# Two empty items between the first one-hots and the first tile of each compaction in a two-layer graph kernel

## The chip, the cores and the metric

The kernel runs on one core of a Trainium2 chip. Its time is the device time of one execution in microseconds (us), and the profile used here is one execution recorded by the hardware profiler. Engines are named as in the profile: PE is the matrix engine (PEld its weight loads), DVE the vector engine, ACT the scalar engine, POOL the general engine (GpSimd), SP the engine that issues most DMAs. A line number such as L612 is a line of the kernel before the change.

## The reference, cut to what matters

Two layers work on x (3327 nodes, 128 features) and a sparse weighted adjacency matrix of 3327 x 3327. The first layer multiplies by the normalised matrix and its transpose and normalises each row. The second is attention with an adjacency bias, and takes nearly all of the time:

```python
q = (x @ Wq.T).reshape(d, n, h)          # d = 128 heads, n = 3327, h = 8
k = (x @ Wk.T).reshape(d, n, h)
v = (x @ Wv.T).reshape(d, n, h)
a = jnp.einsum('dnh,dmh->dnm', q, k) * scale
a = a + spatial_encoding + edge_encoding  # both are adj
a = jax.nn.softmax(a, axis=2)
out = jnp.einsum('dnm,dmh->dnh', a, v)
out = out.reshape(n, h * d) @ Wo.T
x = layernorm(x + out)
```

So there are 128 independent heads, each with a 3327 x 3327 score matrix of inner length 8, an exponential of every score, and a product with 8 values and a row of ones.

## The kernel before, in words

**The main loop.** The heads go in 32 groups of four (g = 0 to 31). For each group the loop at L1396 takes 7 blocks of up to 512 queries and, in each, 26 tiles of 128 keys. The unit of the loop is a *half*: PE makes the scores of two heads for one tile and one block (L1416, tile `e_ps`), ACT takes their exponentials (L1436, tile `es`; L1438 for the last block, where one exponential takes all four heads), and PE multiplies the exponentials of the tile before by the values (L1364, tile `o`). A group has 6 x 52 + 26 = 338 halves, the whole loop 10,816. Every half has one exponential, so the loop runs at best at the pace of ACT.

**What runs beside it.** The maximum of each score row, needed ahead of the exponentials, is not computed from all 3327 keys. The keys of largest norm are picked (a top 1024 and a further 1024) and packed densely; PE multiplies queries by the packed keys and DVE takes maxima. This work of the group ahead is cut into *items*, a stream written by `stream_of` (L929). An item is one of:

- "maxima": two matmuls (L1034) and two DVE maxima over 512 columns (L1043);
- "queries": rebuilds a few query rows for the second 1024 keys (L1018, L1027);
- "hots" and "fill", the *compaction* of the packed keys for the next group, written by `fills` (L766). A "hots" item makes four one-hot tiles with DVE (L612, bf16, 128 x 336). A "fill" item multiplies a tile of keys by four one-hots on PE (8 matmuls, L621), and then makes the four one-hots of the tile after the next on DVE. So two sets of one-hots always lie ahead. A compaction has two "hots" items and 30 "fill" items, the first 15 for the first 512 packed keys, the other 15 for the second 512. There are 30 compactions, one for each of groups 2 to 31, each running while the group before is in the main loop;
- None: an empty item, which takes its place in the stream and emits nothing. Before the change these stand only where the stream has to wait, most of them beside group 30, which has no compaction.

**Pacing.** `next_item` (L1335) takes one item of the stream. Before each half the loop compares the number of items taken with `due(halves)` (L1390), a straight line through the points in `wanted` (L1385), whose slope comes from the number of items of a group. When an item is due (`busy`, L1426), the half carries it, its PE work between the scores and the exponential. When it is not, the half instead lets the small generators in `running` take a step (`turn`, L974), and may let the slow background work take a step (`next(beside)`, L1458; `next(choosing)`, L1456). After the first groups a busy half lets none of these step. So the number of items, empty ones included, decides how many steps the background work gets.

**The background work.** `choosing` selects the keys of largest norm for later groups (beside groups 1 to 6). `beside` runs `neighbours` (L1064) and then `closing` (L1203). `neighbours` treats the exact scores along the edges, node tile by node tile (26 tiles): it gathers rows with indirect DMAs (L1084), takes inner products on DVE (L1094, L1098), then exponentials on ACT, and then on POOL, for each of up to 16 neighbours, a product of gathered values with a share (L1152 for the first neighbour, L1155 for the others) and a sum (L1156). I call such a product with its sum a *value product*. `closing` finishes one tile of 128 output rows at a time (26 tiles): it loads the sums, scales them (L1254 to L1285), transposes them (L1293), multiplies by Wo (L1307) and normalises. What is left of `beside` when the main loop ends runs after it (L1465), with nothing else to do.

POOL's other large job is in `fix` (L809): eight masked products over queries for each pair of heads (L848, then sums L853 to L858).

**Order.** The order of instructions on PE, ACT, DVE, POOL and SP is exactly the order in which this Python code emits them (L1333). Each engine runs its own list in order and waits only for data and buffers, so POOL can be ahead of the loop or behind it. Steps of `beside` cost credits in units of a half (`spend`, `earn`), with which the code keeps DVE and POOL from falling far behind.

Of the kernel before, what the change touches and what calls it, by code (L numbers as in the profile page):

```python
# [52 lines left out]
TCUTS = TOP // NB  # L53
# [10 lines left out]
POOL_BEHIND = 4.0  # L64
DEEPEST = 12.0
READY = 500
MARGIN = 60


def window(t):  # L70
    return EXPECTED * t // NT - BEFORE
# [7 lines left out]
def gnn_layers(ctx: ExitStack, tc: tile.TileContext, x, adj, adjt, w_in, w_out, wq, wk, wv, wo, out):  # L79
# [89 lines left out]
    with ExitStack() as c0:  # L169
# [435 lines left out]
        def tiles_of_fill(u):  # L605
            return [t for t in range(NT) if window(t) < (u + 1) * NB and window(t) + REACH > u * NB]
# [27 lines left out]
        def spread(g, packed):  # L634
            pairs = coming["s", g] = []
            for j in range(GH):
                x, y = j // 2, j % 2
                for slot, parts in KROWS:
                    r = 64 * (1 - y) + H * slot
                    pairs.append((k_kept[g % 2][r : r + H * parts, x, :], packed[32 * j : 32 * j + H * parts, :]))  # L640
# [103 lines left out]
    with c_att as c1:  # L744
# [21 lines left out]
        def fills(g, at, parts):  # L766
            packed = side.tile([P, KEPT], BF16, name="packed")
            state = {}
            order_of = [(u, t) for u in range(TCUTS) for t in tiles_of_fill(u)]
            yield "hots", g, at, order_of[0][1], state  # L770
            yield "hots", g, at, order_of[1][1], state
            for (u, t), after in zip(order_of, [*order_of[2:], None, None]):
                tiles = tiles_of_fill(u)
                yield "fill", g, at, parts, packed, u, t, after, t == tiles[0], t == tiles[-1], state
            spread(g, packed)
# [153 lines left out]
        def stream_of():  # L929
# [13 lines left out]
            parts = split_keys(side, coming_keys[1])  # L943
            maxima_of(2, 1)
            yield from fills(2, coming_keys[0], parts)
            yield from of_rest(1, 0)
            yield from of_rest(1, 1)
            yield from of_top(2, 0)
            for g in range(2, NG):
                if g + 1 < NG:  # L950
                    coming_keys = load_choice(side, g + 1)
                    maxima_of(g + 1, 0)
                yield from of_top(g, 1)
                if g + 1 < NG:
                    maxima_of(g + 1, 1)
                    parts = split_keys(side, coming_keys[1])
                    yield from fills(g + 1, coming_keys[0], parts)
                else:
                    for _ in range(30):
                        yield None  # L960
                yield from of_rest(g, 0)
                if g + 1 < NG:
                    yield from of_top(g + 1, 0)
                else:
                    for _ in range(40):
                        yield None
                yield from of_rest(g, 1)
# [365 lines left out]
        with tc.manual_schedule(engines={ENG.PE, ENG.Activation, ENG.DVE, ENG.Pool, ENG.SP}):  # L1333
# [47 lines left out]
            total = halves = 0  # L1381
            steps = NT * (2 * len(BLOCKS) - 1)
            top, rest = NT * TCUTS, 2 + ROOM * (KCUTS - TCUTS)
            fill = 2 + sum(len(tiles_of_fill(u)) for u in range(TCUTS))
            wanted = [(0, taken), (2 * steps - MARGIN, taken + 4 * top + 4 * rest + 2 * fill + top)]  # L1385
            for g in range(3, NG):
                wanted.append((steps * g - MARGIN, wanted[-1][1] + 2 * (top + rest) + fill))
            wanted.append((steps * NG - MARGIN, wanted[-1][1] + 40))

# [6 lines left out]
            for g in range(NG):  # L1396
                for b, (n0, w) in enumerate(BLOCKS):
# [9 lines left out]
                    for t in range(NT):  # L1407
                        pt = P if t < NT - 1 else P - (NP - N)
                        e = [None] * GH
                        for x0 in range(0, 2, per):  # L1410
# [41 lines left out]
                            if not busy and t and credit["dve"] > 0:  # L1452
                                if halves >= READY and len(chosen_all) < len(LATE):
                                    if "fill" not in held:
# [250 lines left out]
```

## Time and profile before

| what | value |
|---|---|
| median of 3 runs (12162.31 to 12165.54) | 12163.84 us |
| the profiled execution, own time | 12176.24 us |
| its span in the profile | 12174.6 us |
| first and last start of an exponential (L1436, L1438) | 1226.0 us, 12096.4 us |
| end of the main loop's exponentials | 12097.6 us |
| median distance between starts of exponentials | 0.92 us |
| sum of what these distances have over 0.92 us | 920 us |
| ACT es, L1436, x9984 | 9476.1 us busy |
| DVE one-hots, L612, x3840 | 1302.7 us busy, 406 ns mean |

The profiled execution is 12.4 us (0.1%) longer than the median. The distances are those between the starts of successive exponentials in the trace: 10,816 of them, in the order in which the kernel emits them, so each can be put to its half, group and item. In a group without special trouble (groups 7 and 8) they sum to 14.9 us over 338 x 0.92 us.

### The profile page before, as it was taken

The numbers are of one execution on the slowest core, as the hardware profiler recorded it, in microseconds if no ns is written. First come the engines' busy times: TensorE is split into PE (matmuls) and PEld (weight loads), VectorE is DVE, ScalarE is ACT, GpSimd is POOL, SyncE is SP. The second block draws the span as 40 slices with busy tenths as digits, with TensorE's granted clock in tenths as the row PEclk, the third lists the DMA queues.
The fourth block names the chain that finished last, engine by engine and source line by source line (L and its number), as shares of the span: only waits on it lengthen the run. The fifth ranks groups of instructions, "written<-read, shape, count | busy, mean of one in ns | idle before, by whom it ended". The sixth has DMA issues, their size and how long they took to land.

```text
span 12174.6 us, 238129 instructions
## 1 busy us (share of the span) xinstructions
PE 11268.4 (93%) x90213; PEld 2996.4 (25%) x90246; DVE 9384.3 (77%) x18234; ACT 10771.0 (88%) x11299; POOL 3377.5 (28%) x4098
## 2 busy tenths in 40 slices
PE   6647999999999999999999999999999999999997
PEld 3321222222222222222222222222222222222222
DVE  9678787878787788788888887887888778777533
ACT  6431899999999999999999999999999999999996
POOL 0221111111111124444433334334343434211100
PEclk8765999999999999999999999999999999999998
DMA  6562444344441123222222222322222222233112
GB/s 231 159 161 67 40 42 41 37 37 38 39 38 23 19 58 76 61 56 61 61 65 64 64 52 64 72 56 70 60 55 61 62 65 65 62 86 65 35 47 57
DMA packets 2237807, 783.23 MB, mean 64 GB/s; under 512 B 1854432, under 2 KB 2128355, under 8 KB 2229989
## 3 DMA queue, kind: packets, MB, share of 16 engines
q1 hardware_dynamic: 2154085, 436.67, 23.2%
q0 software_dynamic: 78816, 286.92, 7.4%
q10 hardware_dynamic: 3744, 44.29, 1.0%
q8 instruction: 712, 11.67, 0.4%
q14 instruction: 450, 3.69, 0.1%
HBM read 595.42 MB, written 187.86 MB: 64 GB/s over the span
## 4 chain that ended last, share of the span: by engine, by line
ACT 36%; PE 35%; DVE 13%; issue 13%; DMA 1%; SPq 1%; POOL 0%; ACTq 0%; DVEq 0%; POOLq 0%
ACT es L1436 34%; PE o L1364 17%; PE e_ps L1416 11%; DVE mx_top L1043 4%; PE m L1034 3%; DVE mx_rest L1043 1%; DVE hot L612 1%; DVE top_at L256 1%; ACT es L1438 1%; DVE top_w L255 1%; PE acc L246 1%; PE pr L693 1%; PE m L1307 1%; DVE o_sb L1373 1%; PE m L1189 0%
## 5 line engine op out<-in xcount | busy, mean ns | idle before, releaser
L1436 ACT ACTIVATE es<-e_ps 128x1024 f32<-128x1024 f32 (+1 forms) x9984 | 9476.1, 1023 | 729.4 <-PE e_ps L1416 446.7
L1364 PE MATMUL o<-es,v 128*9 128x512 f32 x46592 | 5766.4, 567 | 32.7 <-DVE o_sb L1373 32.2
L1043 DVE TENSOR_REDUCE mx_top<-m 128x1 f32<-128x512 f32 x6656 | 4255.7, 685 | 1200.6 <-PE m L1034 1178.9
L1416 PE MATMUL e_ps<-q_e,k_st 50*128 50x512 bf16 (+1 forms) x23296 | 4271.8, 371 | 227.3 <-ACT es L1436 77.2
L1416 PEld LDWEIGHTS <-k_st 50*128 50x128 bf16 (+1 forms) x23296 | 1408.3, 95 | 6261.3 <-issue 5780.4
L1043 DVE TENSOR_REDUCE mx_rest<-m 128x1 f32<-128x512 f32 x2048 | 1309.6, 684 | 356.3 <-PE m L1034 352.6
L1034 PE MATMUL m<-k_kept,q_m 48*128 48x512 bf16 x6656 | 1434.0, 386 | 110.4 <-DVE mx_top L1043 62.0
L612 DVE TENSOR_SCALAR hot<-hot_no,at 128x336 bf16<-128x336 bf16 x3840 | 1302.7, 406 | 221.6 <-PE m L621 205.5
L848 POOL TENSOR_TENSOR slot_each<-hits,whole_q 128x832 f32<-128x832 f32 x256 | 425.6, 1663 | 2893.1 <-DVE hits L833 2878.0
L1364 PEld LDWEIGHTS o<-es,v 128*9 128x9 f32 x46592 | 696.3, 88 | 1563.8 <-issue 1447.1
L1438 ACT ACTIVATE es<-e_ps 128x1020 f32<-128x1020 f32 x832 | 810.5, 1024 | 78.2 <-PE e_ps L1416 60.9
L1034 PEld LDWEIGHTS <-q_m 48*128 48x128 bf16 x6656 | 509.0, 144 | 159.0 <-issue 152.7
L1084 POOL DMA_INDIRECT near_rows<-kn_d,near x211 | 201.4, 954 | 1069.6 <-DVE prod L1094 1004.8
L1034 PE MATMUL m<-k_kept,slot_rows_q 48*128 48x512 bf16 x2048 | 443.1, 385 | 34.5 <-DVE mx_rest L1043 27.6
L802 POOL TENSOR_TENSOR slot_each<-whole_q 128x416 f32<-128x416 f32 x64 | 57.4, 897 | 1429.3 <-DMA whole_q<-qf_d 1378.2
L1156 POOL TENSOR_TENSOR acc<-acc,prod 128x1024 f32<-128x1024 f32 x185 | 430.3, 2326 | 14.5
L246 PE MATMUL acc<-a_t,x 128*128 128x512 f32 (+1 forms) x728 | 311.5, 585 | 63.0 <-DMA a_t<-in_adj_dram 43.0
L1155 POOL TENSOR_TENSOR prod<-near_rows,s 128x1024 f32<-128x1024 f32 x185 | 365.9, 1978 | 2.4
L621 PE MATMUL m<-hot,parts 128*24 128x168 bf16 (+9 forms) x7200 | 289.8, 230 | 40.5 <-DVE hot L612 40.2
L1084 POOL DMA_INDIRECT near_rows<-vn_d,near x211 | 206.9, 980 | 345.6 <-DVE prod L1094 295.6
L1094 DVE TENSOR_TENSOR prod<-qn,near_rows 128x512 f32<-128x512 f32 x422 | 296.2, 702 | 0.0
L853 POOL TENSOR_TENSOR slot_each<-slot_each 128x416 f32<-128x416 f32 x256 | 288.1, 1125 | 20.1
(308 smaller groups left out, 5914.5 us busy)
## 6 DMA issues: line engine op xcount, KB each, us to landing
q_m<-q_d SPq DMA_DIRECT2D x768, 52.0 KB
q_e<-q_d SPq DMA_DIRECT2D x2304, 16.0 KB
a_t<-in_adj_dram ACTq DMA_DIRECT2D x13, 1663.5 KB
a_t<-in_adj_dram SPq DMA_DIRECT2D x13, 1663.5 KB
a_t<-in_adjt_dram SPq DMA_DIRECT2D x13, 1663.5 KB
a_t<-in_adjt_dram ACTq DMA_DIRECT2D x13, 1663.5 KB
q_d<-parts SPq DMA_DIRECT2D x13, 1536.0 KB
k_d<-parts SPq DMA_DIRECT2D x13, 1536.0 KB
```

The source lines that it names most:

```text
L246: nc.tensor.matmul(acc[:, b, :w], x0[:, t, :], a_t[:, n0 : n0 + w], start=t == 0, stop=t == NT - 1)
L612: nc.vector.tensor_scalar(hot, hot_no, at[:, t, j : j + 1], None, op0=ALU.is_equal)
L848: nc.gpsimd.tensor_mul(each, hits[y][:, i : i + 4, :, None].to_broadcast(shape), whole_q[:, y, None].to_broadcast(shape),)
L1034: nc.tensor.matmul(banks[y], of[rows[y], tile_of], kept[rows[y], x, c * NB : (c + 1) * NB], start=True, stop=True,)
L1043: nc.vector.tensor_reduce(mx[:, i, y, c - c0 : c - c0 + 1], banks[y], axis=AX.X, op=ALU.max)
L1084: nc.gpsimd.indirect_dma_start(rows.rearrange("p d h -> p (d h)"), None, table, bass.IndirectOffsetOnAxis(ap=rows_at, axis=0))
L1155: nc.gpsimd.tensor_mul(prod, vg, share)
L1156: nc.gpsimd.tensor_add(acc[:, :, :H], acc[:, :, :H], prod)
L1364: nc.tensor.matmul(o[32 * j : 32 * j + VW, :w], v4[:pt, j, t, :], e[j][:pt], start=t == 0, stop=t == NT - 1,)
L1416: nc.tensor.matmul(bank[:pt, y, x * NB // per : x * NB // per + w], k[r, x0 + x, t * P : t * P + pt], q[r, x0 + x, :w], start=True, stop=True,
L1436: nc.scalar.activation(es[:pt, :, :w], bank[:pt, :, :w], AF.Exp, scale=2.0)
L1438: nc.scalar.activation(es[:pt].rearrange(shape, x=per)[:, :, :, :w], bank[:pt].rearrange(shape, x=per)[:, :, :, :w], AF.Exp, scale=2.0,)
```

## The change

Between the two "hots" items and the first "fill" item of each compaction, two empty items are put into the stream. The count `fill`, from which the due times are worked out, grows from 32 to 34, so that the line `wanted` allows for them. The instructions of the program are the same in number on every engine; their order among each other changes.

```diff
+CATCH_UP = 2
...
         yield "hots", g, at, order_of[0][1], state
         yield "hots", g, at, order_of[1][1], state
+        for _ in range(CATCH_UP):
+            yield None
         for (u, t), after in zip(order_of, [*order_of[2:], None, None]):
...
-            fill = 2 + sum(len(tiles_of_fill(u)) for u in range(TCUTS))
+            fill = 2 + CATCH_UP + sum(len(tiles_of_fill(u)) for u in range(TCUTS))
             wanted = [(0, taken), (2 * steps - MARGIN, taken + 4 * top + 4 * rest + 2 * fill + top)]
             for g in range(3, NG):
                 wanted.append((steps * g - MARGIN, wanted[-1][1] + 2 * (top + rest) + fill))
```

## The prediction, made before the result was known

> **What bounds the kernel now.** I read the page first, then the engine table in windows, then the trace exponential by exponential. The page:
>
> ```profile
> span 12174.6 us, 238129 instructions
> PE 11268.4 (93%) x90213; PEld 2996.4 (25%) x90246; DVE 9384.3 (77%) x18234; ACT 10771.0 (88%) x11299; POOL 3377.5 (28%) x4098
> L1436 ACT ACTIVATE es<-e_ps 128x1024 f32<-128x1024 f32 (+1 forms) x9984 | 9476.1, 1023 | 729.4 <-PE e_ps L1416 446.7 <-DMA q_e<-q_d 246.4 <-PE m L1034 1.8
> L612 DVE TENSOR_SCALAR hot<-hot_no,at 128x336 bf16<-128x336 bf16 x3840 | 1302.7, 406 | 221.6 <-PE m L621 205.5
> L1155 POOL TENSOR_TENSOR prod<-near_rows,s 128x1024 f32<-128x1024 f32 x185 | 365.9, 1978 | 2.4
> L1156 POOL TENSOR_TENSOR acc<-acc,prod 128x1024 f32<-128x1024 f32 x185 | 430.3, 2326 | 14.5
> ```
>
> PE shows the larger share, but its matmuls overlap. The exponentials set the pace: they start 0.92 us apart whenever nothing is late, and 10,816 of them need 9951 us. The 920 us above that are stalls of the loop, and only these, and what runs after the loop, can be changed by moving items.
>
> Next, the engines during the second half of a compaction (from the start of the group's half 52 to that of half 90), for six of the head groups. Columns: window, length, busy time and instructions by engine, granted PE clock, DMA share, GB/s.
>
> ```profile
> 5061.50:5111.50 50.00, 43.78 (x386) 9.65 (x381) 36.04 (x69) 36.67 (x39) 29.39 (x28) 0.83 0.29 97
> 5403.50:5454.60 51.10, 42.21 (x384) 10.12 (x382) 39.85 (x69) 36.92 (x39) 34.65 (x31) 0.90 0.32 105
> 5746.70:5789.10 42.40, 38.79 (x387) 9.05 (x382) 29.56 (x74) 36.29 (x39) 19.06 (x23) 0.92 0.27 90
> 6084.70:6121.10 36.40, 36.06 (x387) 8.92 (x382) 28.46 (x85) 36.08 (x39) 7.81 (x16) 1.00 0.25 70
> 7078.60:7139.30 60.70, 46.85 (x384) 10.55 (x382) 54.45 (x69) 37.47 (x39) 52.44 (x41) 0.83 0.33 106
> 9072.70:9119.60 46.90, 40.60 (x383) 9.86 (x382) 36.06 (x69) 37.49 (x41) 36.39 (x35) 0.93 0.25 71
> ```
>
> The same 38 halves take 36.4 us when POOL is busy for 7.81 us (group 14) and 60.7 when it is busy for 52.44 (group 17). The reader is to see that the length follows POOL, the fifth busy time, though nothing in a compaction waits for POOL's results. The value products (L1155) in three of these windows:
>
> ```profile
> 5061.50:5111.50 50.00, 7.90 (x4) 0.83 0.29 97
> 6084.70:6121.10 36.40, 0.00 (x0) 1.00 0.25 70
> 7078.60:7139.30 60.70, 15.81 (x8) 0.83 0.33 106
> ```
>
> What is slow is the one-hot. In the window of group 17 the 62 one-hots have a mean of 893 ns; in the like window of group 16 (6749.5 to 6786.0 us, POOL busy 9.69 us) 63 have 359 ns. The waits in the window of group 17 name PE m L621 behind DVE hot L612 with 13.6 us and ACT es behind PE e_ps with 23.1 us. So a value product beside a compaction slows the one-hots, PE waits for them in order, and ACT waits for PE. Value products beside maxima show no such stall: in groups 9 to 27 a maxima half has 0.11 us over 0.92 with one beside it and 0.10 without.
>
> **The price of one overlap.** With L1152 counted, 4, 5, 2, 9, 2 and 6 value products fall in the windows of groups 11, 12, 13, 17, 20 and 23, which exceed 36.4 us by 13.6, 14.7, 6.0, 24.3, 3.7 and 10.5: together 72.8 us for 28 products, 2.6 each, between 1.75 (group 23) and 3.4 (group 11). Other windows have none and no excess worth the name.
>
> A rule of the Trainium skill bears on this (SBUF — State Buffer, section "Who interferes with whom"): a DVE instruction in a two-port mode, which a tensor_scalar can enter, and a GpSimd instruction lock each other out of a shared port pair for the whole instruction. The rows agree in kind (359 against 893 ns). If each overlap cost the whole of its two POOL instructions, 1.98 + 2.33 us, the 24 further overlaps found below would cost 103 us in place of 62; the measured 2.6 decides.
>
> **The change, part by part.**
>
> *The empty items themselves.* Empty items already stand beside group 30, and such a half is 0.92 us like any other. Sixty more cost nothing on an engine.
>
> *What they were placed for.* The first "fill" after the one-hots shows 0.38 + 0.14 us over 0.92, the same in nearly every group. That goes: -0.52 us a group.
>
> *A denser stream.* In groups 2 to 29 a group takes 174 items in place of 172 in 338 halves, so more busy halves stand next to each other. By the two built orders, each group gets one more run of three maxima halves (the third costs 0.84 us in groups 7, 8 and the like), one run of three fills (0.20 to 0.30 in groups 0 and 1) and one pair after two empty halves (0.2), and loses a pair at its end (0.28). With the 0.52 that is 0.84 + 0.25 + 0.2 - 0.28 - 0.52 = +0.5 us, 14 us for 28 groups. In groups 0 and 1 the runs exist already: nothing. Bounds: -15 us (only the first fill moves) and +40 us (each run at its dearest, a run of fills at 0.84 too).
>
> *Background steps lost.* The 62 more busy halves take steps from `beside`: 2320 in place of 2363 by the built orders. That has two consequences.
>
> First, the tail. 118 steps are left at the end of the loop in place of 75, which is two more tiles of `closing`, each run alone. The chain of work after the loop:
>
> ```profile
> 12106.28 11.55 issue
> 12117.83 1.94 PE m L1293 x8
> 12119.77 3.57 PE m L1307 x16
> 12123.34 11.02 issue
> ...
> 12140.03 11.38 issue
> ```
>
> From 12106.28 to 12123.34 and on to 12140.03 a tile takes 17.1 and 16.7 us; with the DVE starts of L1254 (12108.55, 12125.08) 16.5. Two tiles are +33, and one product (L1275, 1.22 us) more is left of the tile in work: +34. What hides them today is the loop, where they are not free: group 31, nearly all closing tiles, has 52.3 us over 0.92 a half, for some 12 tiles, at most 4.3 a tile. Two fewer there give back up to 8. Net +26, bounds +20 and +34.
>
> Second, and larger, the steps of `neighbours` come later against the compactions, and this drifts by a few steps a group. I counted where value products fall. Rule: POOL finishes `fix` at about half 57 (seen in groups 11, 12, 13 and 17), then runs the products that the order gives it up to the end of the node tile, one in 5.65 us (L1155 starts at 7093.70, 7099.33, 7105.01), whether or not the loop has got there; if the tile's sums begin later, from there. This rule finds the six counts of before. In the changed order it finds products beside ten compactions: groups 11: 5, 12: 7, 13: 5, 14: 3, 18: 4, 20: 8, 22: 6, 25: 6, 26: 5, 27: 3. That is 52 for 28: 24 more, at 2.6 each **+62 us**. Bounds: 24 x 3.4 = 82 above; below, if half of the 22 products in groups 20, 25, 26 and 27, which depend on POOL running ahead, miss the fills, 13 x 2.6 = 34. I take 62, the mean price over all 28 cases.
>
> The two empty halves do not cover this. They put DVE ahead at half 28; the loss arises after half 57, and the one-hots stay two sets ahead, as before.
>
> *The rest.* The key selection has the same number of steps (439), and its three pairs of rank passes move by a few halves: nothing, within 10 us either way. SP and ACT get the same lists in nearly the same places.
>
> **Sum** against the profiled execution: 12176.24 + 62 + 26 + 14 = 12278. The median stands 12.4 us below that execution, so 12163.84 + 102 = **12266 us**. By the bounds, 34 + 20 - 15 = +39 to 82 + 34 + 40 = +156: 12203 to 12320.
>
> **Rivals.**
> - *The one-hots' lead swallows the stalls (faster).* If the two empty items gave DVE a lead that lasts, the 72.8 us of the six groups would go and no new overlap would cost anything: -73 + 26 + 14 = -33, 12131 us. For it: PE waits for one-hots, and the change gives them time. Against it: the lead is four halves, 3.7 us, the backlog in group 17 is 24 us, and it arises 25 halves later. It decides from the point where a lead carries to half 57. 0.06.
> - *The overlaps do not grow.* POOL's place in time is not its place in the order; if products slip out of the fills as often as in, only tail and density are left: +40, 12204 us. 0.15, two thirds of it over 0.2%.
> - *The overlaps cost more than before*: products following each other through a whole compaction, with the clock at 0.83 as in group 17; over 12320 us. 0.06.
> - *It does nothing measurable*: fewer overlaps than today pay for the tail, within 24 us. 0.04.
>
> **How the numbers follow.** The forecast has 0.69. A measurement of this kernel can tell about 0.2% (24 us) from no change. Faster: 0.06. Within: 0.05 + 0.04 = 0.09. Slower: 0.69 + 0.10 + 0.06 = 0.85. The range, 12192 to 12318, holds most of the forecast and of the second rival.
>
> **What the profile after would show.** Windows of the second half of the compaction at 45 us or more in about ten groups (among them 18, 22 and 25, at 36.4 today) and 36.4 in the others; the mean of all one-hots up from 406 ns; five closing tiles after the last exponential in place of three, that stretch 111 us in place of 77; the first fill without its 0.5 us. I am wrong if groups 18, 22 and 25 stay at 36.4 us, or if a group with value products beside its compaction does.

## The result, and the profile after

The changed kernel takes **12313.34 us** (median of 3 runs, 12310.05 to 12313.83) against 12163.84: ratio 1.0121, 95% interval 1.0108 to 1.0135, or 149.5 us more. The forecast was 12266 (12192 to 12318), so the sign was right, the time lies in the range, 5 us below its upper end, and the forecast was 47 us too low.

In the page of the changed kernel a line up to the edit of `fills` has a number higher by 1, a line behind it by 3 (L612 is L613, L1436 is L1439):

```profile
span 12308.3 us, 238547 instructions
...
L1439 ACT ACTIVATE es<-e_ps 128x1024 f32<-128x1024 f32 (+1 forms) x9984 | 9490.1, 1025 | 829.3 <-PE e_ps L1419 544.7
L613 DVE TENSOR_SCALAR hot<-hot_no,at 128x336 bf16<-128x336 bf16 x3840 | 1377.0, 428 | 255.4 <-PE m L622 242.5
```

The exponentials are busy for about the same time (9476.1 us before), and two numbers have moved: the one-hots' mean went from 406 to 428 ns, and ACT now waits 100 us longer in front of the exponentials.

The difference of the two profiled executions (133.7 us of span) can be laid out by the starts of the exponentials (all in us; "excess" is what the distances between starts have over 0.92 us a half):

| where | before | after | difference | predicted |
|---|---|---|---|---|
| start of the loop | 1226.0 | 1221.3 | -4.7 | 0 |
| excess, groups 0 to 8 | 314.9 | 312.2 | -2.7 | +3 |
| groups 9 to 27, halves 0 to 54 | 40.7 | 44.4 | +3.7 | +10 with the line after next |
| groups 9 to 27, halves 54 to 92 (second half of the compaction) | 101.5 | 161.3 | **+59.8** | **+62** |
| groups 9 to 27, halves 92 to 338 | 303.4 | 325.6 | **+22.2** | (in the +10) |
| groups 28 to 31 | 159.9 | 181.0 | **+21.1** | **-8** |
| after the last exponential's end | 77.0 | 111.5 | +34.5 | +34 |

The rest, 15.7 us, is that the profiled execution stood 12.4 us above its median before and stands 3.3 below it after. (The +3, +10 and part of groups 28 and 29 are the predicted 0.5 us a group.)

The engines in the second half of the compaction, first for groups 18 and 22 of the kernel before, then for groups 11, 17, 18, 22 and 25 of the changed kernel (there the stretch is taken two halves later, from half 54 to half 92, as the two empty items stand ahead of it). The columns are those of the prediction: window, length, busy time of PE, PEld, DVE, ACT and POOL with their instructions, granted PE clock, DMA share, GB/s.

```profile
7430.40:7466.80 36.40, 36.05 (x387) 8.89 (x381) 29.62 (x88) 36.11 (x39) 9.77 (x18) 1.00 0.32 98
8745.80:8782.20 36.40, 36.06 (x388) 8.94 (x382) 29.15 (x88) 36.08 (x39) 8.95 (x18) 1.00 0.29 85
```

```profile
5055.70:5105.70 50.00, 41.91 (x388) 9.56 (x382) 37.95 (x71) 36.86 (x40) 29.93 (x19) 0.86 0.32 108
7093.20:7130.60 37.40, 36.46 (x388) 9.22 (x382) 24.59 (x74) 37.07 (x41) 13.12 (x16) 1.00 0.06 12
7422.10:7470.40 48.30, 40.95 (x388) 9.64 (x382) 34.73 (x71) 36.74 (x38) 28.40 (x25) 0.89 0.30 100
8781.40:8836.40 55.00, 46.12 (x388) 10.16 (x382) 43.66 (x72) 37.12 (x39) 39.71 (x33) 0.81 0.33 107
9791.00:9841.60 50.60, 42.28 (x386) 9.92 (x380) 40.78 (x71) 36.88 (x38) 35.31 (x24) 0.90 0.33 106
```

Group 17, which was the worst with 60.7 us, is down to 37.40, and group 23 to 36.40; groups 18, 22 and 25, quiet at 36.4, take 48.30, 55.00 and 50.60. The length again follows POOL's work there, the fifth busy time. The value products (L1158) in groups 17 and 22:

```profile
7093.20:7130.60 37.40, 0.00 (x0) 1.00 0.06 12
8781.40:8836.40 55.00, 11.88 (x6) 0.81 0.33 107
```

None and six. In all ten groups that the prediction names, the trace has the predicted number of products, 52 in sum. The other groups from 9 to 27 have none but one late product in group 17, and no window above 37.5 us. The chain of work after the loop:

```profile
12207.23 10.92 issue
12218.15 1.94 PE m L1296 x8
...
12222.79 11.87 issue
...
12273.42 11.52 issue
```

Five closing tiles stand behind the last exponential, each with a wait of 11 to 12 us (the others begin at 12239.56 and 12256.39), one every 15.6 to 17.0 us. Before the change there were three.

### The profile page after: what moved, and what is told of

Its sections match the earlier page's. It is cut to its first block, busy times and chain, and to the rows that moved or that the text cites. A ratio compares the mean times of both kernels' runs of the same rounds, so it can differ in the third digit from the quotient of the medians.

```text
span 12308.3 us, 238547 instructions
## 1 busy us (share of the span) xinstructions
PE 11319.0 (92%) x90246; PEld 2998.5 (24%) x90246; DVE 9468.8 (77%) x18234; ACT 10783.7 (88%) x11299; POOL 3392.4 (28%) x4098
## 4 chain that ended last, share of the span: by engine, by line
PE 43%; ACT 29%; issue 10%; DVE 9%; DMA 1%; SPq 0%; POOL 0%; ACTq 0%; DVEq 0%; POOLq 0%
ACT es L1439 25%; PE o L1367 21%; PE e_ps L1419 14%; PE m L1037 5%; DVE mx_top L1046 3%; ACT es L1441 3%; DVE mx_rest L1046 1%; DVE hot L613 1%; PE m L622 1%; DVE o_sb L1376 1%; PE m L1310 1%; PE m L1192 0%; DVE above L477 0%; PE m L1296 0%; DVE slot_rows_q L1030 0%
## 5 line engine op out<-in xcount | busy, mean ns | idle before, releaser
L1439 ACT ACTIVATE es<-e_ps 128x1024 f32<-128x1024 f32 (+1 forms) x9984 | 9490.1, 1025 | 829.3 <-PE e_ps L1419 544.7
L613 DVE TENSOR_SCALAR hot<-hot_no,at 128x336 bf16<-128x336 bf16 x3840 | 1377.0, 428 | 255.4 <-PE m L622 242.5
L1159 POOL TENSOR_TENSOR acc<-acc,prod 128x1024 f32<-128x1024 f32 x185 | 432.0, 2335 | 14.5
L1158 POOL TENSOR_TENSOR prod<-near_rows,s 128x1024 f32<-128x1024 f32 x185 | 366.4, 1980 | 2.4
L622 PE MATMUL m<-hot,parts 128*24 128x168 bf16 (+9 forms) x7200 | 299.9, 230 | 67.2 <-DVE hot L613 66.7
L1376 DVE COPY o_sb<-o 128x512 f32<-128x512 f32 (+1 forms) x224 | 145.4, 649 | 197.8 <-PE o L1367 192.9
```

Of the source, the lines that this page charges most:

```text
L613: nc.vector.tensor_scalar(hot, hot_no, at[:, t, j : j + 1], None, op0=ALU.is_equal)
L622: nc.tensor.matmul(banks[which][32 * j : 32 * j + PARTS * H, lo - u * NB : hi - u * NB], parts[:, j * NT + t].rearrange("p s h -> p (s h)" ...
L1158: nc.gpsimd.tensor_mul(prod, vg, share)
L1159: nc.gpsimd.tensor_add(acc[:, :, :H], acc[:, :, :H], prod)
L1439: nc.scalar.activation(es[:pt, :, :w], bank[:pt, :, :w], AF.Exp, scale=2.0)
```

## The experiments

Theory: the empty items do nothing themselves; they make halves busy, so the steps of `beside` come later; value products then meet the one-hots of more compactions, and closing tiles are left for the end. First rival: the denser stream itself costs it. Second rival: it is not POOL's products but the gathers' traffic beside them.

Beside experiments 1 to 11 the kernel before takes 12238 to 12247 us, beside experiment 12 it takes 12163, as in the first measurement. So each is given as a ratio to the kernel before measured along with it, and its parts against those of e9_before_again (the kernel before, unchanged, at 12240 us). "Beside the compactions" is the sum for halves 54 to 92 of groups 9 to 27, as in the table.

**1. The empty items without the displaced steps.** The kernel with the change, but the steps of `beside` are taken in exactly the halves in which the kernel before takes them (a list worked out ahead):

```diff
-                                elif halves >= START and credit["pool"] > 0:
-                                    next(beside, None)
+                            if halves in STEPS:
+                                next(beside, None)
```

> The items of the changed kernel, empty ones included, with every step of the background work (beside) pinned to the half in which the kernel before takes it: the order of value products against one-hots is that of before (28 overlaps by the counting rule), and 75 steps are left at the end as before. Theory (the displaced background costs the time, the empty items hardly any): 12178 us, 12165 to 12205, two closing tiles fewer after the loop than in the changed kernel, windows of groups 18, 20, 22, 25 back at 36.4 us, those of 17 and 23 long again. Rival (the empty items and the denser stream cost it): about 12310 us.

Ratio 1.0006 (0.9996 to 1.0016); beside the compactions 120.8 us (kernel before: 123.1), behind the loop 76.1. Groups 17, 18 and 22:

```profile
7088.00:7149.00 61.00, 47.40 (x387) 11.04 (x382) 53.97 (x71) 37.39 (x38) 49.30 (x33) 0.83 0.33 105
7442.30:7479.70 37.40, 36.07 (x387) 8.89 (x382) 29.93 (x92) 36.30 (x39) 6.33 (x9) 1.00 0.32 96
8782.20:8819.40 37.20, 36.18 (x389) 9.03 (x382) 29.80 (x91) 36.30 (x39) 4.96 (x5) 1.00 0.26 83
```

The long and the short windows are those of the kernel before. The items themselves and the denser stream cost about 7 us by the ratio, which is not told from nothing. In the one profile, groups 0 to 27 outside these stretches have 11.2 us more than in experiment 9 (718.9 against 707.7).

**2. The displaced steps without the empty items.** The kernel before with the same edit, its list being the halves in which the changed kernel takes a step.

> The items of the kernel before, no empty ones added, with every background step pinned to the half in which the changed kernel takes it: 49 overlaps by the counting rule, 118 steps left at the end. Theory: nearly all of the change's cost without the change: +60 us of overlaps, +34 us after the loop and some 20 to 45 us of other collisions of the same steps, 12290 us (12260 to 12315). Rival (the empty items cost it): about 12164 us.

Ratio 1.0105 (1.0088 to 1.0122); beside the compactions 211.0 us, behind the loop 111.1, groups 28 to 31 175.2. The same three groups:

```profile
7116.10:7153.60 37.50, 36.38 (x383) 9.35 (x377) 25.00 (x72) 37.17 (x42) 13.40 (x21) 1.00 0.09 18
7447.60:7499.90 52.30, 42.74 (x383) 9.97 (x377) 36.13 (x69) 36.88 (x40) 29.38 (x28) 0.87 0.28 94
8822.20:8881.70 59.50, 47.20 (x384) 10.28 (x378) 44.80 (x69) 37.40 (x40) 40.40 (x35) 0.83 0.31 101
```

Without a single empty item, group 17 is quiet and 18 and 22 are long (25 too, with 55.1 us), as in the changed kernel. Together the two runs show the cause of nearly all of the loss: it is where the background steps fall. The share of the compactions differs, though: here the steps cost 87.9 us there (211.0 less 123.1), with 52 products in the windows as in the changed kernel, and 59.8 in the first pair of profiles. Part of that is something else: the windows of groups 10 and 24 hold no product in either and take 42.6 and 41.4 us here, where the changed kernel took 36.4 and 36.7. What lengthens these is open.

**3 and 4. One-hots that do not contend with POOL.** The Trainium skill (VectorE: DVE Perf Modes, section "What auto-detection actually checks") ties a two-port mode to the outermost dimensions of source and destination being both even or equal. So the index tile gets 21 rows of 16 in a stride of 17. What is computed is the same, but the outermost sizes are now 21 in the source and 336 in the destination, where both were 336.

```diff
-        hot_no = early.tile([P, 2 * REACH], BF16, name="hot_no")
+        hot_no = early.tile([P, 21, 17], BF16, name="hot_no")[:, :, :16]
-            nc.vector.tensor_copy(hot_no, hot_i)
+            nc.vector.tensor_copy(hot_no, hot_i.rearrange("p (a b) -> p a b", b=16))
...
-                nc.vector.tensor_scalar(hot, hot_no, at[:, t, j : j + 1], None, op0=ALU.is_equal)
+                nc.vector.tensor_scalar(
+                    hot.rearrange("p (a b) -> p a b", b=16), hot_no, at[:, t, j : j + 1], None, op0=ALU.is_equal
+                )
```

In the changed kernel:

> The changed kernel with the one-hots read from an index tile of 21 rows of 16 in rows of 17, so that source and destination have outermost sizes 21 and 336 instead of 336 and 336; same result, same order. Theory (a one-hot is slow beside a value product because both need something exclusive that only the fast form of the instruction takes): one-hots alone a little slower than the 302 ns median, but the same with and without value products beside them; the windows of the second half of a compaction go to 36 to 38 us in all groups, the kernel to about 12185 us (12160 to 12215). Rival (memory traffic, the gathers or the clock slow the one-hots): windows as long as before or longer, 12313 us or more.

In the kernel before:

> The kernel before with the same other form of the one-hots, no empty items. Theory: its six long windows go to 36 to 38 us as well, 73 us less, about 12095 us (12075 to 12125), so that the empty items cost some 90 us with this form (after the loop, and collisions outside the compactions) in place of 149. Rival (the form only makes one-hots slower): 12164 us or more.

Ratios 1.0031 (1.0018 to 1.0044) and **0.9954 (0.9937 to 0.9971)**. The second beats both kernels of the change. The one-hots in the stretch of group 22, in the changed kernel (8781.4 to 8836.4) and then in experiment 3 (8771.4 to 8812.4), where the engines of that stretch follow:

```profile
L613 DVE TENSOR_SCALAR hot<-hot_no,at 128x336 bf16<-128x336 bf16 x65 | 39.9, 684 | 4.1 <-PE m L622 3.0 <-PE e_ps L1419 1.1
```

```profile
L613 DVE TENSOR_SCALAR hot<-hot_no,at 128x336 bf16<-128x336 bf16 x64 | 20.6, 392 | 5.2 <-PE m L624 5.2
```

```profile
8771.40:8812.40 41.00, 37.69 (x399) 9.39 (x393) 24.71 (x72) 36.25 (x39) 36.29 (x26) 1.00 0.36 112
```

POOL is busy for 36.29 of 41.00 us, six value products among it, and the one-hots take 392 ns: no one-hot of the run takes more than 0.41 us (2.65 in the changed kernel), and the window lasts 41.0 in place of 59.5 (experiment 2). What it still has over 36.4 is no one-hot: at its end DVE waits once for 4.7 us and ACT for 3.3, and the profile puts both down to "remote", a releaser that is not one of the core's engines. The price is a one-hot of 390 ns always, where the plain form has a median of 302 and a tail of up to 2.65 us. Beside the compactions the changed kernel falls to 71.5 us and the kernel before to 54.5: of the 88 us between them (211.0 less 123.1, experiments 2 and 9) 17 are left. One part of the expectation was missed: four of the six windows of the kernel before keep 41 to 43 us, where 36 to 38 was expected. Behind the loop nothing changes (110.8 against 77.2), nor in groups 28 to 31 (179.2 against 159.7).

The skill (SBUF — State Buffer, section "Who interferes with whom") says that a DVE instruction with at most one SBUF input and outside the two-port modes does not contend with GpSimd. The run agrees: no one-hot of this form is above 0.41 us. What a meeting costs in the plain form was the measured price: after the change the ten windows with products exceed 36.4 us by 133.6 us for 52 products, 2.57 each (predicted 2.6), not the 4.3 us that the two POOL instructions last.

**5 and 6. Moving the steps the other way.** `START`, the half at which `beside` begins, from 3000 to 2600 and to 2700, in the kernel before:

```diff
-START = 3000
+START = 2600
```

> The kernel before, items unchanged, with the background work started at half 2600 in place of 3000 (one constant). Theory: only the place of the background steps against the compactions and what is left at the end count. The counting rule finds 23 overlaps in place of 28 (-13 us at 2.6 each), 27 steps are left in place of 75, some 2.3 closing tiles of 16.6 us fewer after the loop (-38) and as many more in it (+10): -41 us against before, ratio 0.9966 (0.994 to 1.000). Rival (only the amount of empty or waiting items matters, the phase of the background does not): -28 us from the tail alone, as for the start at 2700.

> The same with the start at half 2700. The counting rule finds 64 overlaps (+36, +94 us at 2.6 each), 27 steps are left as for 2600 (-38, +10): +66 us against before, ratio 1.0054 (1.002 to 1.009), and some 105 us longer than with the start at 2600. Rival (phase does not matter): as for 2600, a ratio near 0.998.

Ratios 1.0024 (1.0014 to 1.0033) and 1.0057 (1.0040 to 1.0074). The second lies in its range (196.3 us beside the compactions, with 65 products in the trace where the rule counted 64), but it is 48 us longer than the first, where 105 was expected. The first missed. The stretch behind the loop falls to 43.3 us, near the expected gain, but beside the compactions it has 128.0, about what the kernel before has: the trace has 28 products there, as many as before, and not the 23 of the rule. And halves 92 to 338 grew from 349.8 to 409.0, against 24 us won in groups 28 to 31. Of these 59 us, 43 lie in halves 256 to 297 (67.2 to 110.2), where DVE merges a group's maxima: of its merge instructions (L898 to L911, with medians of 0.20 to 0.56 us) 35 take more than 1.5 us in groups 9 to 27, and 13 in experiment 9. So most of the growth looks like a second kind of meeting, which is shown with the denser stream below; no run tried it by itself.

**7 and 8. Without the products.** POOL's product and sum for all neighbours but the first are left out and replaced by a memset of one element (the weighted sum over neighbours is not computed), in the changed kernel and in the kernel before:

```diff
-                        nc.gpsimd.tensor_mul(prod, vg, share)
-                        nc.gpsimd.tensor_add(acc[:, :, :H], acc[:, :, :H], prod)
+                        nc.gpsimd.memset(prod[:, :1, :1], 0.0)
```

> The changed kernel without the products and sums of gathered values of all neighbours but the first (the two POOL instructions of each; the output lacks these contributions); the gathers and every other instruction stay in their order, with a tiny POOL memset in place of each product. Theory: all long windows go to 36 to 38 us, as do the collisions outside the compactions, and against before the kernel has left the longer stretch after the loop and the denser stream: ratio to the kernel before 0.998 to 1.001. Rival (gathers or memory traffic slow the one-hots): windows stay long, 1.012.

> The kernel before with the same POOL instructions left out (the output lacks the same contributions). Theory: its six windows go to 36 to 38 us, ratio to before about 0.993 (0.990 to 0.996). What the changed kernel without products takes more than this one is what the change costs without any collision of value products: 34 us after the loop, 5 to 25 us of denser stream, and -8 us (my prediction) or +20 us (what the changed kernel's profile shows) in groups 28 to 31.

Ratios 1.0083 (1.0066 to 1.0100) and 1.0007 (0.9997 to 1.0017): both missed. The one-hots' mean falls to 374 and 379 ns, yet the long windows keep 41 to 49 us. The edit changes a second thing: without POOL's arithmetic the gathers often follow each other at 1.25 us (80 of the 210 gaps between value gathers are under 1.4 us in experiment 7, none in the changed kernel). Five us of the compaction of group 22 in the first of the two:

```profile
8812.00:8817.00 5.00, 2.44 (x10) 0.33 (x10) 0.00 (x0) 0.57 (x1) 2.65 (x3) 0.50 1.01 400
```

```profile
DVE hot L613 <- remote: 10.4, 3, 6.6
ACT es L1438 <- remote: 10.3, 2, 5.6
```

DVE does nothing and ACT one instruction, the DMA engines are full (share 1.01, 400 GB/s), and the releaser of both is again "remote". In the whole run such waits sum to 90 us on ACT and 119 on DVE, against 12 and 19 in experiment 9. So these runs say nothing on the products; what exactly the engines waited for stays open.

**9. The kernel before again**, unchanged, for the parts at 12240 us:

> The kernel before, unchanged, for a second profile of it on the chip of these experiments: by both theories its time, and the same long windows (groups 11, 12, 13, 17, 20, 23). It tells which of the stalls outside the compactions belong to the chip and not to the order.

Ratio 1.0001 (0.9991 to 1.0011). Its long windows are those of the first profile (groups 11, 12, 13, 17, 20, 23); the excess of the loop is 990.8 us in place of 920.6, 46 us of it in halves 92 to 338, and groups 28 to 31 are alike to 0.1 us. What makes that difference is open. It need not be the chip: chip number 5 stands in the record with 12241 us once (experiments 5 to 8) and with 12163 once (experiment 12). One sign stands in the traces: waits put down to "remote" are in none of the three profiles at the shorter times (before, after, experiment 12) and in all eleven of the others, here 30 us on DVE and ACT together.

**10. The products without the gathers.** In the changed kernel the value rows are not gathered; the products read the query rows that are there (so the sums are of other data):

```diff
-                for table in (kn_d, vn_d):
+                for table in (kn_d,):
...
-                    vg = gather()
+                    vg = qn
```

> The changed kernel without the gathers of neighbours' values (the products take the query rows instead, so the output is wrong in these contributions); the products and sums on POOL stay, in the same order. Theory (the POOL instructions themselves hold up the one-hots): long windows and slow one-hots stay in groups 11 to 14, 18, 20, 22, 25 and 26, ratio to before 1.008 to 1.016. Rival (the gathers' traffic does it, as the stalls of the kernels without products would suggest): windows go to 36 to 38 us, ratio about 1.000.

Ratio 1.0121 (1.0104 to 1.0138), beside the compactions 203.7 us. Groups 18 and 22:

```profile
7447.90:7498.70 50.80, 41.31 (x389) 9.23 (x382) 31.83 (x71) 36.78 (x39) 22.05 (x14) 0.90 0.22 75
8824.00:8882.00 58.00, 46.35 (x388) 9.86 (x382) 40.48 (x71) 37.05 (x39) 34.95 (x28) 0.76 0.20 65
```

The traffic falls by a third (group 22: 65 GB/s in place of 101 in experiment 2) and the windows are about as long. So in the windows with products the second rival falls: POOL's products hold up the one-hots, not the gathers of the values. (The gathers of the keys, ahead of the products, stay in this run, and so do the 42.5 and 41.7 us of groups 10 and 24.)

**11. Other form and earlier start together**, to see whether the shorter end adds to the gain of experiment 4:

> The kernel before with the other form of the one-hots and the start of the background work at half 2600: the tail of 27 steps (-34 us) without the slow one-hots. Theory: the form takes the price of the overlaps whatever their number, so that the earlier start keeps its gain after the loop: ratio to before 0.990 to 0.996, below the 0.9954 of the form alone. Rival (the earlier start costs the loop as much as it saves behind it, whatever the one-hots): 0.997 to 1.000.

Ratio 0.9983 (0.9974 to 0.9993): behind the loop 43.7 us and beside the compactions 64.5, but halves 92 to 338 at 415.8. That is the rival's range: the earlier start costs in the loop more than it saves behind it, and experiment 4 stays the best kernel.

**12. The changed kernel again**, unchanged:

> The changed kernel unchanged, on chips of the kind on which the kernel before takes 12240 us, where its stalls in halves 54 to 92 of groups 9 to 27 sum to 123.1 us, in halves 92 to 338 to 349.8, in groups 28 to 31 to 159.9, with a stretch of 75.3 us behind the last exponential. Theory (the displaced background steps cost the time, beside the compactions and behind the loop, whatever the chip): ratio 1.010 to 1.014, halves 54 to 92 at 195 to 215 us, stretch behind the loop 111, groups 28 to 31 at 173 to 182. Open is only the growth of halves 92 to 338, 22 us in the first pair of profiles: if it comes from value products beside small DVE operations of the merge, it shows here too, 365 to 375 us; if it belongs to that pair of profiles, 345 to 355. The kernel with the items of before and the background steps of the changed one had 350.5, so the rival has the better chance, unless the denser stream and the steps cost it together.

Ratio 1.0116 (1.0099 to 1.0133), 12304.87 against 12163.29 us: the kernel before took the shorter time again, so the expectation's question about the longer one stays unanswered by it. It repeats the first profile part by part: 160.6 beside the compactions, 323.9 in halves 92 to 338, 179.2 in groups 28 to 31, 111.6 behind the loop. So the rows of the table are not chance. In the pair of experiments 2 and 9 the row of halves 92 to 338 does not grow (350.5 against 349.8), though the same meetings and the same longest stall stand in it (next section).

## Why the prediction was right or wrong, point by point

**Empty items cost nothing: right** (experiment 1, 1.0006).

**24 more overlaps at 2.6 us, +62: right.** The counts hold in all ten groups, the price is 2.57, and +59.8 us was measured. (At 12240 us the same steps cost 87.9 us there, so the price is that of this pair of profiles.) One detail was off: the three products of group 27 fall late in the compaction (halves 79, 83 and 89) and cost nothing, 37.3 us. Experiments 2, 3 and 10 show the mechanism: displaced steps, products on POOL, one-hots held up.

**Two more closing tiles behind the loop, +34: right**, 34.5 (experiment 1: 76.1 us, experiment 2: 111.1).

**"Two fewer there give back up to 8": this step failed.** Groups 28 to 31 rose by 21.1 us. Group 31, on which the step was argued, did give back (52.3 to 50.5), but group 29 went from 29.8 to 45.0 and group 28 from 46.2 to 50.8. I moved tiles in number only, and not the stretch of work ahead of them: 91 of the transposes at the end of `neighbours` (L1192, L1189 before, after its sums) now fall in group 29, where there were 25, and of the four closing tiles that started their DVE work there two are left, the second at half 300, among maxima. The waits of the changed kernel from 11434 to 11456 us (us in total, times, longest):

```profile
ACT es L1439 <- PE e_ps L1419: 8.0, 3, 5.8
DVE prod L1257 <- DMA prod<-flatmax_d: 7.1, 1, 7.1
PE m L1037 <- DVE mx_top L1046: 5.6, 1, 5.6
```

To be read from the middle line: DVE, in order, holds a product of the closing tile (L1257, L1254 before) that waits 7.1 us for its DMA; behind it stand the maxima, behind these PE, behind PE the exponential. That one half has 5.9 us of excess. It shows in experiments 2, 3 and 12 too (6.0, 6.0, 6.1) and in none of experiments 1 and 4, so it comes with the displaced steps. Why the DMA is late can be read on SP: it issues the stores of the group's maxima one after another from 11419.39 to 11439.76 us, the last (L926) for 7.30, and the tile's load only at 11441.02. (The kernel before has a tile behind the same stores, but there DVE comes to its product 11 us after the load was issued, 11350.51 to 11361.48, and does not wait.) Of the rest of group 29's 15 us, 9 lie in halves 60 to 180, beside the transposes; that was read from the profile and not tried by itself.

The same queue makes the longest stall of the changed loop, in group 27. The transposes of `neighbours` began in half 152 of that group before, and begin in half 293 now, just when SP issues the stores of the maxima:

```profile
10707.61 7.29 SPq L926 DMA_DIRECT2D flatmax_d<-negative  x1
10715.14 0.34 SPq L1175 DMA_DIRECT2D acc<-nn_d  x1
10719.93 1.10 PE L1192 MATMUL m<-ident,acc 128*128 128x128 f32 x4 [12.28 <-DMA acc<-nn_d]
10723.40 1.03 ACT L1439 ACTIVATE es<-e_ps 128x1024 f32<-128x1024 f32 x1 [14.35 <-PE e_ps L1419]
```

PE, in order, stands for 12.28 us before a transpose whose load is issued behind the stores, and ACT for 14.35. The stall is in experiments 2, 3, 7, 10 and 12 (14.5 to 14.9 us of excess in that half) and not in the kernel before or experiments 1, 4, 8 and 9. It stands in the row of halves 92 to 338; as group 27 has 66 transposes fewer than before, its sum there rises by 4.3 us only. A shorter wait of PE for the same kind of load, 2.9 us, stands in group 28 at half 305 and is part of that group's rise.

**The denser stream, +14: near in size, and hides other things.** Groups 0 to 27 outside the windows rose by 23.2 us. Some 12 of these are not density but value products beside the small DVE operations at about half 279, the merge of a group's maxima: groups 15, 18 and 22 rose by 24.0 us in halves 92 to 338, groups 14 and 23, which had such a meeting before, fell by 12.1 (in experiment 2 against 9: +29.9 and -12.8, the same groups). In group 18 of the changed kernel (start, us):

```profile
7655.36 0.27 DVE L913 TENSOR_TENSOR two_group<-negative,two_group 128x104 bf16<-128x104 f32 x1
7655.66 2.52 DVE L914 TENSOR_TENSOR negative<-two_group 128x104 f32<-128x104 bf16 x1
...
7656.07 1.97 POOL L1158 TENSOR_TENSOR prod<-near_rows,s 128x1024 f32<-128x1024 f32 x1
```

The sum L914 takes 2.52 us beside a product of POOL; the median of the 32 sums of this line is 0.27. In group 22 it is three other instructions of the merge that take 2.0 to 2.3 us beside products. The prediction asked whether products hurt one-hots and maxima, and left out the third kind of DVE work. Another 4.3 us are the net rise of group 27. What is then left to density is about 7 us; experiment 1, which has the density without the displaced steps, has 11.2. One term of it was wrong: the stall of the first fill (-0.52 us a group) did not go. It stands four halves later, with 0.14 and 0.34 us in place of 0.14 and 0.38 (means of groups 9 to 27).

**The sum**: 149.5 less 102 is 47.5: 29 from groups 28 to 31, 9 from density, merge and group 27 together, 15.7 from taking the profiled execution's distance to the median as fixed, and -6 from the start of the loop, the overlaps and the tail. The rivals: no lead swallowed the stalls (group 17 went quiet because its products went elsewhere), overlaps grew as counted, and in this pair of profiles their price stayed. That the total still fell into the range owes something to luck: +29 us in groups 28 to 31 came from a path that was not in the bounds.

## What to carry to other kernels

An item that does nothing was free here on every engine and still moved all work that is paced by counting items. So ask first what slides, and then, place by place, what it slides beside. Count the meetings of instructions that hold each other up, with one price per meeting and over all kinds of instructions of the engine that is held up. Then follow the slid work to its end: look for its first instructions that wait for a DMA on an engine with urgent work behind it, and for what stands ahead of that DMA in its queue. Where the meetings cost more than a slower instruction would, try another form of the instruction in place of another schedule: a one-hot that is 88 ns slower alone but never held up was worth 0.46%, more than any placement tried here.

## What the runs showed of the hardware that was not expected

- A bf16 compare of 128 x 336 with outermost sizes 21 and 336 takes 390 ns (median, experiment 3), at most 410, whether POOL works or not; the plain form has a median of 302 ns and 440 of 3840 over 0.6 us, the longest 2.65 (changed kernel). Without the value products 334 are still over 0.6 us (experiment 7), so POOL's other work may hold up one-hots too.
- Gathers that follow each other every 1.25 us (DMA share 1.01, 400 GB/s) stood beside waits of up to 6.6 us on DVE and 5.6 on ACT, on a releaser outside the core's engines (experiment 7). Whether the gathers cause them is not shown.
- The same program took 12163 us at some times and 12240 at others, with 70 us more of stalls in the loop (990.8 against 920.6), and kept its pattern of long and short windows.
- SP issued the six stores of a group's maxima one after another for 20 us (10694.48 to 10714.90 in the changed kernel), and a load behind them held PE for 12.28 us.
